# Two padded bias vectors fetched in four strided requests each instead of sixteen

## The chip, the cores and the metric

The kernel runs on one core of one Trainium2 chip. The metric is the device time of that core in microseconds (us), as the median of several runs. The profile comes from one further execution; its span and its own time are given beside the median.

## The reference

Two layers, each an attention over a context followed by a routed feed-forward part, work on `x` (4 batches, 512 tokens, 256 features) and a context of the same shape. All values are 32-bit floats. Cut to its frame:

```python
x = x + _L0_xattn_ref(_layernorm(x), ctx, ctx, ...)   # attention over probability vectors, then an MLP of 1024
x = x + _L0_ffn_ref(_layernorm(x), ...)               # 8 experts of 1024, the best two of each token
x = x + _L1_xattn_ref(_layernorm(x), ctx, ctx, ...)   # 16 heads of 16 features
x = x + _L1_ffn_ref(_layernorm(x), ...)               # 8 experts of 512, the best one of each token
```

The two vectors of this case belong to the third line:

```python
qw = split_heads(q @ Wq + bq)
kw = split_heads(k @ Wk + bk)
```

Each has 256 entries, 16 for each of 16 heads.

## The kernel before, in words

Tokens lie on the 128 partitions, four to a partition for each batch. At the start the function loads x and context of batch 0, the weights and biases that the first stages need, and then the other batches, one request after the other on the queue of SyncE (SP): `load_batch(0)`; `packed("Wk_pad")` and `rows("L1_xattn_Wv")` (L124); `packed_column("bk_pad")` and the bias of values (L125); `load_batch(1)` (L126); `WdT`, `b_diff`, the columns of the layer norm, the MLP's weights `w1_mlp` and `w2_mlp`, further biases, and batches 2 and 3 (L127 to L139). A later group, `load_later` (L141 to L152), loads what only layer 1 uses: `Wq_pad`, `packed_column("bq_pad")`, `wo` in 16 requests of 16 rows (L150), `w_red` and `wg` (L151).

On the host the biases are laid out for heads of 32 places: place 0 is kept for something else, places 1 to 16 hold the head's 16 entries, the rest is zero. The padded 512 places are turned into a source of 128 rows and 4 columns, so that head `hd` lies in column `hd // 4`, at rows `32 * (hd % 4) + 1` and on. `packed_column` (L105) brings them into a tile `w` of 128 partitions and 2 columns without the padding. It does so head by head: 16 requests of 16 rows with one element each.

Layer 0 works by batches. `front` (L685) normalizes x (`q`), makes probability vectors of q and of the context (`qp`, `kp`, through L657 to L664), their logarithms (`ql`, `kl`, L666), and the differences (L699, L702); GpSimd (POOL) adds `b_diff` to q (L700). `attend` (L705) transposes the differences on TensorE (`transposed`, L258, with copies at L267 and L269), multiplies them (`pm_sid`, L721), takes the exponential (L722), weighs the context (`pf`, L729) and multiplies by `WdT` (`pd`, L744, added to q as `f` at L745). `perceive` (L748) is the MLP; POOL adds `ln_b` to x (L754) and `b2_mlp` to f (L753). `remember` (L879) is the part of layer 1 that needs only the context: it transposes the context (L899), multiplies by `Wk` (L905), adds the bias of keys on ScalarE (ACT, L906), multiplies by `Wv` (L915), adds the bias of values on VectorE (DVE, L919), and stores keys and values in DRAM (L910, L923). `select_weights` (L809) turns `wg` and `w_red` into the weights of layer 1's selection: four small DVE operations on `wg` (L813, L814, L815, L817) with a power on POOL (L816), and then TensorE. `clear` (L195) fills the DRAM buffers `sent` with rows that go nowhere: 32 stores (L199).

What sets the order: in the first stage (L938 to L951), over batch 0 and the start of batch 1, the order on TensorE (PE), DVE, ACT and POOL is that of the program. From L952 to L987 a scheduler orders the instructions of all engines by its own estimates of times, until the tail of layer 0 and layer 1's attention again fix the order on PE. SP's queue is ordered by the scheduler throughout. Each engine, SP too, works through its own queue in order. A transfer signals its end on one of eight semaphores, which are used in turn; so in the built program a request on SP waits until the eighth request before it has landed.

The bias of queries `bq` is used only in layer 1 (`prepare`, L1128).

Of the kernel before, what the change touches and what calls it, by code (L numbers as in the profile page):

```python
# [21 lines left out]
P = 128  # L22
NT = S // P
NC = D // P
# [3 lines left out]
HEADS, DH = 16, 16  # L28
# [15 lines left out]
def xattn_ffn_kernel(ctx: ExitStack, tc: tile.TileContext, a: dict, out: bass.AP):  # L44
    nc = tc.nc
# [59 lines left out]
    def packed_column(name):  # L105

        w = const.tile([P, NC], F32, tag=name, name=name)
        for hd in range(HEADS):
            c, r = divmod(hd * DH, P)
            g, j = divmod(hd, 4)  # L110
            nc.sync.dma_start(w[r : r + DH, c : c + 1], a[name][32 * j + 1 : 32 * j + 1 + DH, g : g + 1])
        return w

    def load_w1(ap, n):
# [8 lines left out]

    (wk, pack_wk), wv = packed("Wk_pad"), rows("L1_xattn_Wv")  # L124
    bk, bv = packed_column("bk_pad"), spread_row("L1_xattn_bv")  # L125
    load_batch(1)  # L126
    wdT = rows("WdT")  # L127
# [13 lines left out]
    def load_later():  # L141

        w_out, b_out = rows("L0_ffn_W_out"), spread_row("L0_ffn_b_out")
        (wq, pack), bo = packed("Wq_pad"), spread_row("L1_xattn_bo")
        pack()
        bq = packed_column("bq_pad")
        wo = const.tile([P, NC, D], F32, tag="wo", name="wo")
        for hd in range(HEADS):
            c, r = divmod(hd * DH, P)
            nc.sync.dma_start(wo[r : r + DH, c, :], a["Wo_pad"][32 * hd + 1 : 32 * hd + 1 + DH, :])  # L150
        w_red, wg = rows("L1_ffn_w_red", RED), columns("L1_ffn_wg")  # L151
        return w_out, b_out, wq, bo, bq, wo, w_red, wg  # L152
# [525 lines left out]
    with tc.tile_pool(name="l0a", bufs=2) as lp, tc.tile_pool(name="l0tmp", bufs=2) as tp, tc.tile_pool(  # L678
        name="l0mid", bufs=1
    ) as midp, tc.tile_pool(  # L680
        name="l0p_m", bufs=3, space=bass.MemoryType.PSUM
# [276 lines left out]
        for b in range(B):  # L958
# [9 lines left out]
            if b < B - 1:  # L968
# [7 lines left out]
                if b == B - 2:  # L976
                    ((e, row),) = send.pick(1)
                    w = send.weights(e)
# [169 lines left out]
    with tc.tile_pool(name="f0tmp", bufs=2) as tp, tc.tile_pool(  # L1148
        name="f0mid", bufs=2
    ) as midp, tc.tile_pool(  # L1150
        name="f0p_m", bufs=3, space=bass.MemoryType.PSUM
# [31 lines left out]
    with tc.tile_pool(name="l1a", bufs=2) as lp, tc.tile_pool(name="l1s", bufs=1) as sp, tc.tile_pool(  # L1183
        name="l1p_s", bufs=6, space=bass.MemoryType.PSUM
# [268 lines left out]
    with tc.tile_pool(name="f1tmp", bufs=2) as tp, tc.tile_pool(  # L1453
        name="f1mid", bufs=2
    ) as midp, tc.tile_pool(
        name="f1p_m", bufs=3, space=bass.MemoryType.PSUM
# [60 lines left out]
```

## Time and profile before

| | us |
|---|---|
| median of 3 runs | 1018.66 (1017.84 to 1022.89) |
| the profiled execution, its time | 1020.77 |
| the profiled execution, its span | 1019.0 |
| PE busy | 957.3 |
| DVE busy | 530.1 |
| ACT busy | 358.0 |
| POOL busy | 290.9 |
| mean granted clock of PE | 0.979 |
| 16 requests of `bk_pad` on SP | 10.15, from 3.18 |
| 15 of the 16 requests of `bq_pad` on SP | 7.94, from 42.11 |

Times in the text are microseconds from the start of the span. "SPq" is the time that SP's sequencer spends on issuing a request, its waits among it; the landing of a transfer is seen at the first instruction that waited for it. "PEclk" or "granted clock" is the share of its full clock that PE was given. A line of the program stands for all instructions that it makes; `x16` counts them.

### The profile page before, as it was taken

How to read it: one execution, taken by the hardware profiler on the slowest of the kernel's cores; microseconds unless marked ns; L12 is line 12 of the kernel's file. 1: busy time of each engine (PE TensorE's matmuls, PEld its weight loads, DVE VectorE, ACT ScalarE, POOL GpSimd, SP SyncE). 2: the span in 40 equal slices, each digit the busy share in tenths (PEclk: the TensorE clock that was granted, in tenths of full speed). 3: DMA queues.
4: the chain of work that ended last, by engine and by line, in shares of the span. 5: the costliest groups of instructions: out<-in, count | busy, mean ns of one | idle time of the engine just before them, and what ended most of it. 6: DMA issues, size and time to landing. Idle time of an engine off the chain costs nothing. (4 is left out here: it accounts for less than half of the span.)

```text
span 1019.0 us, 14212 instructions
## 1 busy us (share of the span) xinstructions
PE 957.3 (94%) x4885; PEld 645.4 (63%) x4885; DVE 530.1 (52%) x1409; ACT 358.0 (35%) x647; POOL 290.9 (29%) x333
## 2 busy tenths in 40 slices
PE   5979989999898999999999989999999999997996
PEld 3556757676777888888888864343333343346785
DVE  6775595456762222222323158676687777624232
ACT  4535242122121122111222203655656555563231
POOL 3330143325341222211112146306023220123543
PEclk9889999999999999999999999999999999999998
DMA  6779999973333655666655331101011102035672
GB/s 198 232 185 246 249 252 240 246 172 114 130 125 130 212 183 170 206 213 211 230 163 199 123 139 43 27 12 43 5 38 47 43 6 99 37 87 166 203 226 79
DMA packets 113713, 146.05 MB, mean 143 GB/s; under 512 B 15060, under 2 KB 95197, under 8 KB 113632
## 3 DMA queue, kind: packets, MB, share of 16 engines
q1 hardware_dynamic: 106592, 128.19, 44.4%
q0 software_dynamic: 6624, 15.80, 4.8%
q8 instruction: 43, 0.70, 0.3%
q10 hardware_dynamic: 416, 1.05, 0.3%
q14 instruction: 38, 0.31, 0.1%
HBM read 86.71 MB, written 58.80 MB: 143 GB/s over the span
## 5 line engine op out<-in xcount | busy, mean ns | idle before, releaser
L1218 DVE TENSOR_REDUCE nm<-sc 128x1 f32<-128x512 f32 x256 | 165.1, 683 | 61.4 <-PE scT L1211 57.5
L1215 ACT ACTIVATE ex<-scT 128x512 f32<-128x512 f32 x256 | 138.5, 596 | 94.7 <-PE scT L1211 94.0
L634 PE MATMUL pm<-inT,w 128*128 128x256 f32 x736 | 166.9, 382 | 3.1 <-ACT mid L638 2.4
L647 PE MATMUL po<-w,mid 128*128 128x256 f32 x736 | 163.3, 379 | 0.0
L1211 PE MATMUL sc<-kT,qT 32*128 32x512 f32 x512 | 154.5, 650 | 3.8 <-DVEq L626 1.6
L634 PEld LDWEIGHTS pm<-inT,w 128*128 128x128 f32 x736 | 140.1, 192 | 24.5 <-ACT mid L638 4.4
L647 PEld LDWEIGHTS po<-w,mid 128*128 128x128 f32 x736 | 138.0, 190 | 17.8
L1211 PE MATMUL scT<-qT,kT 32*128 32x512 f32 x512 | 148.5, 639 | 0.9 <-ACT ex L1215 0.9
L523 POOL DMA_INDIRECT came<-y,rows x38 | 37.5, 986 | 223.8 <-DVE y L601 223.8
L244 POOL TENSOR_TENSOR rstd<-var,halved 128x4 f32<-128x4 f32 (+1 forms) x32 | 28.1, 883 | 248.9 <-DVE var L243 243.0
L601 DVE SCALAR_TENSOR_TENSOR y<-po,rows,y 128x256 f32<-128x256 f32 x54 | 26.1, 484 | 130.4 <-PE po L647 125.6
L638 ACT ACTIVATE mid<-pm,b 128x256 f32<-128x256 f32 x108 | 49.8, 471 | 110.5 <-PE pm L634 85.5
L1211 PEld LDWEIGHTS sc<-kT,qT 32*128 32x128 f32 x512 | 50.4, 185 | 59.0 <-DVE nm L1218 35.8
L636 DVE TENSOR_SCALAR mid<-pm,b 128x256 f32<-128x256 f32 x76 | 36.8, 484 | 95.5 <-PE pm L634 91.3
L598 ACT ACTIVATE y<-b,rows 128x256 f32<-128x256 f32 x54 | 24.5, 500 | 158.2 <-DMA b<-in_L_ffn_b 125.1
L339 POOL DMA_INDIRECT sent<-rows,slot x48 | 47.4, 987 | 102.6 <-DVE slot L336 62.1
L1232 PE MATMUL av<-ex,va 128*32 128x512 f32 x512 | 68.6, 605 | 0.0
L763 PE MATMUL pm<-hT,w 128*128 128x512 f32 x128 | 62.4, 612 | 0.5 <-DVE hT L676 0.5
L769 PE MATMUL po<-w,mid 128*128 128x256 f32 x256 | 59.2, 381 | 0.0
L769 PEld LDWEIGHTS po<-w,mid 128*128 128x128 f32 x256 | 47.9, 190 | 9.1 <-issue 3.1
L1211 PEld LDWEIGHTS scT<-qT,kT 32*128 32x128 f32 x512 | 45.5, 183 | 6.4 <-issue 4.6
L1232 PEld LDWEIGHTS av<-ex,va 128*32 128x32 f32 x512 | 10.2, 108 | 48.2 <-issue 36.8
(312 smaller groups left out, 1268.4 us busy)
## 6 DMA issues: line engine op xcount, KB each, us to landing
w<-in_L_ffn_W SPq DMA_DIRECT2D x40, 1024.0 KB
sent<-nowhere SPq DMA_DIRECT2D x32, 1161.0 KB
w<-in_L_ffn_W SPq DMA_DIRECT2D x22, 512.0 KB
rows<-sent SPq DMA_DIRECT2D x27, 258.0 KB
b<-in_L_ffn_b SPq DMA_DIRECT2D x28, 128.0 KB
y<-came SPq DMA_DIRECT2D x6, 512.0 KB
x<-in_x SPq DMA_DIRECT2D x4, 512.0 KB
c<-in_ctx SPq DMA_DIRECT2D x4, 512.0 KB
```

What stands on the lines that cost most here:

```text
L339: i = nc.gpsimd.indirect_dma_start(out=sent[self.layer][:, :], out_offset=bass.IndirectOffsetOnAxis(ap=slot[:, t - tts[0], k : k + 1], axi ...
L523: i = nc.gpsimd.indirect_dma_start(out=came[self.layer][:, :], out_offset=bass.IndirectOffsetOnAxis(ap=rows[:, u, TO:ROW].bitcast(I32), ax ...
L634: nc.tensor.matmul(pm, w1[:, c, ts(k, P)], inT[:, c, :], start=c == 0, stop=c == NC - 1)
L636: nc.vector.tensor_scalar(mid[:, k, :], pm, bias[:, k : k + 1], 0.0, ALU.add, ALU.max)
L638: nc.scalar.activation(mid[:, k, :], pm, func, bias=bias[:, k : k + 1])
L647: nc.tensor.matmul(po, mid[:, k, ts(t, P)], w2[:, k, :], start=k == 0, stop=k == n - 1)
L763: nc.tensor.matmul(pm, w1_mlp[:, c, ts(k, P)], hT[:, c, :], start=c == 0, stop=c == NC - 1)
L769: nc.tensor.matmul(po, mid[:, k, ts(t, P)], w2_mlp[:, k, :], start=k == 0, stop=k == HD // P - 1)
L1211: nc.tensor.matmul(sc, stay, move, start=True, stop=True)
L1215: nc.scalar.activation(ex, sc, AF.Exp, scale=1.0 / DH**0.5)
L1218: nc.vector.tensor_reduce(nm[:, t, head, 0:1], sc, AX.X, ALU.max, negate=True)
L1232: nc.tensor.matmul(av[32 * head : 32 * head + 32, :], vas[b % 2][:, t, 4 * g + head, :], exs.pop((t, head)), start=t == 0, stop=t == NT - 1,)
```

## The change

The source is seen as columns `c` and halves `g`, and each request takes the 64 rows that go to one half of one column of the tile: for each of four heads (`j`) its 16 entries (`r`, places 1 to 16). One request so has 64 rows of one element, four requests make a bias, and `bk_pad` and `bq_pad` are both fetched in this way. The 256 elements and the tile are the same.

```diff
         w = const.tile([P, NC], F32, tag=name, name=name)
-        for hd in range(HEADS):
-            c, r = divmod(hd * DH, P)
-            g, j = divmod(hd, 4)
-            nc.sync.dma_start(w[r : r + DH, c : c + 1], a[name][32 * j + 1 : 32 * j + 1 + DH, g : g + 1])
+        of_heads = a[name].rearrange("(j r) (c g) -> c g j r", r=32, g=2)
+        for c in range(NC):
+            for g in range(2):
+                nc.sync.dma_start(w[64 * g : 64 * g + 64, c : c + 1], of_heads[c, g, :, 1 : 1 + DH])
         return w
```

In the built program PE and ACT keep their order. On SP four requests stand where sixteen stood, and the store of values of batch 1 (L923), which stood behind fifteen of the sixteen `bq_pad` requests, now stands behind the four and eleven of the `wo` requests. On DVE the operations L813, L814, L815 and L817 move from around L799 to L806 to the place behind the last L664 of batch 2's `kp`, among the four L745 of batch 1; one bn_stats of batch 2 (L241), its aggregate and the variance (L243) move the other way, to behind L805. On POOL, L816 moves ahead of the two operations that stood before it.

## The prediction, made before the changed kernel was run

> **What bounds the kernel now.** I read the page first, then the sums by 20 us stretches, then the timelines of SP, PE, DVE, ACT and POOL over the first 80 us, the waits of PE, and last the order of the instructions in the two built kernels. On the page PE is the bound:
>
> ```profile
> span 1019.0 us, 14212 instructions
> PE 957.3 (94%) x4885; PEld 645.4 (63%) x4885; DVE 530.1 (52%) x1409; ACT 358.0 (35%) x647; POOL 290.9 (29%) x333
> ```
>
> A change to small loads can only win where PE stands still, and over the span PE waits for a transfer three times: twice for context (12.0 us together: 7.2 at the start, 4.8 here) and once for routed rows (2.8 us, at 313 us, far from this change). The 4.8 us lie directly behind the biases of keys. The timeline of SP's queue (start, duration, issue, count):
>
> ```profile
> 1.27 0.70 SPq L64 DMA_DIRECT2D c<-in_ctx  x1
> 2.67 0.47 SPq L78 DMA_DIRECT2D L_xattn_Wv<-in_L_xattn_Wv  x1
> 3.18 10.15 SPq L111 DMA_DIRECT2D bk_pad<-in_bk_pad  x16
> ...
> 13.84 0.43 SPq L63 DMA_DIRECT2D x<-in_x  x1
> 14.32 0.57 SPq L64 DMA_DIRECT2D c<-in_ctx  x1
> 14.93 0.62 SPq L78 DMA_DIRECT2D WdT<-in_WdT  x1
> 15.59 0.82 SPq L90 DMA_DIRECT2D L_xattn_b_diff<-in_L_xattn_b_diff  x1
> ```
>
> Sixteen requests hold SP for 10.15 us, and from 8.5 to 13.5 us the DMA engines are 0.04 busy. The context of batch 1 is asked for at 14.32 and PE gets it at 21.54, as PE's timeline shows (in brackets the idle time before, and who ended it):
>
> ```profile
> 13.14 3.62 PE L915 MATMUL pv<-L_xattn_Wv,kc 128*128 128x256 f32 x16
> 21.54 1.94 PE L899 MATMUL psTr<-ident,c 128*128 128x128 f32 x8 [4.79 <-DMA c<-in_ctx]
> 23.28 1.92 PE L263 MATMUL psTr<-ident,qp 128*128 128x128 f32 x8
> 25.87 1.97 PE L263 MATMUL psTr<-ident,ql 128*128 128x128 f32 x8 [0.68 <-ACT dT L267]
> 27.77 3.42 PE L721 MATMUL pm_sid<-dT,lT 128*128 128x512 f32 x4
> ```
>
> **Part 1, the biases of keys.** Twelve requests of 10.15 / 16 = 0.63 us go: 7.6 us of SP. Not all of it comes through. In the built program every request on SP waits for the landing of the eighth before it (the trace shows such waits: 1.4 us for the context and 1.0 us for Wk among the sixteen). So x of batch 1 is now held by context 0, which landed at about 7.1 (ACT began on it at 7.10), and context 1 by Wk (POOL began on it at 8.48). Context 1 is thus issued at 8.5 in place of 14.3, and with the same 7.2 us to landing it is there at 15.7, before PE's pv ends at 16.76. The 4.79 us wait goes.
>
> What is late next is DVE. Its rows for batch 0: L699 ends at 19.54, L702 at 20.67, two L919 at 21.87; only then comes the copy of dT (0.69), to 22.6. The eight transposes of ql need that buffer: 1.9 us, to 24.5, and pm_sid starts there in place of 27.77. First gain: **3.3 us**, not 4.8.
>
> Part of it is given back by something the trace shows one batch later:
>
> ```profile
> 39.09 3.24 DVE L664 TENSOR_SCALAR kp<-kp,pr_r 128x256 f32<-128x256 f32 x4
> ...
> 39.71 2.47 POOL L700 TENSOR_TENSOR q<-q,L_xattn_b_diff 128x1024 f32<-128x1024 f32 x1 [2.88 <-ACT qp L657]
> ```
>
> The same four DVE operations take 1.14 us at 12.60 and at 16.05; under a POOL add they take 3.24. Today the first such add (b_diff onto q of batch 0) waits 10.2 us for its data, to 22.71, and meets only copies out of PSUM, which keep their 0.69. With b_diff issued at about 9.7 and landing 5 to 7 us later (now 7.1), the add starts between 14.7 and 16.8 and falls on L661 to L664 of qp (15.63 to 17.19). Everything from there to dT waits for its end: add at 14.7: 1.4 us; at 15.6: 2.3; after 17.2: nothing. Bounds 0 and 2.4, taken 1.8. So **1.5 us** are left of 3.3.
>
> A rule and a row for the clock. From 20.5 to 30.5 the granted clock was 0.50, which is why four pm_sid matmuls took 3.42 us. The Trainium skill, "TensorE: Matmul & The Clock Gate", Part 1, says that an idle stretch of about 3.4 us halves the clock: by it, closing the gap keeps the clock, and ql's transposes (0.9) and pm_sid (1.7) would win 2.6 us more. But the row says that transposes do not hold it: they ran from 21.54 to 27.7 with the clock at 0.50 throughout, and Part 4 of the page says the same of transpose mode. Between pv and pm_sid there are only transposes in either kernel, so I take no gain; 2.6 stays as the far end. There is a loss too: the clock came back at 30.7, 2.9 us after pm_sid began; if it comes back at fixed instants, as five drops (20.4, 64.8, 136.8, 194.8, 314.0) lying multiples of about 3.4 us apart suggest, an earlier pm_sid works longer at half clock. Plus or minus 1.7 us (half of 3.4), taken as 0.
>
> **The new requests themselves** (64 rows of one element) have no row. Near ones: requests of 128 rows were issued in 0.33 (b_mlp_col) to 0.71 us (ln_b_col), those of 16 in 0.31 to 0.65, so issue does not grow with the rows: 0.5 taken, bounds 0.3 and 2.5 (four times 0.63). The skill's "DMA: Bandwidth & Descriptors", section "Why a DMA increments its semaphore by 16 and not by 1", speaks against the change: a request is spread over the largest number up to 16 that divides the outer dimension of both sides. Source 4 x 16 against 64 rows gives 4 DMA engines with 16 elements each, where a 16-row request had 16 with one each. The row: ten old requests in 5 us at 0.04 busy on 16 engines are 3.2 us of engine time for 160 elements, 0.02 us each; 16 in a row are 0.3 us and all 64 of a bias on one engine 1.3. By the row that is hidden: the first use (ACT L906 at 11.63) comes 2 to 3 us after their landing behind Wv. Cost 0, at most 1.
>
> **Part 2, the biases of queries.** They are first used at 566 us; only the queue behind them matters:
>
> ```profile
> 42.11 7.94 SPq L111 DMA_DIRECT2D bq_pad<-in_bq_pad  x15
> 50.15 0.37 SPq L923 DMA_DIRECT2D values<-room  x1
> ...
> 51.04 8.08 SPq L150 DMA_DIRECT2D wo<-in_Wo_pad  x16
> ...
> 59.63 0.42 SPq L84 DMA_DIRECT2D L_ffn_wg<-in_L_ffn_wg  x1
> ```
>
> Twelve go at 0.53: 6.3 us. The store of values now stands behind eleven of the wo requests instead of fifteen bq; it waits for DVE (room L919, ends 48.88), which is 1.5 earlier. The 32 clearing stores begin at about 51 in place of 60.16 and last 150 us; no compute engine waits for them on the page, so this is worth nothing.
>
> The built order holds one surprise: the scheduler moves the four small DVE operations on wg (and POOL's power of them, L816) from about 67 us to just after L664 at 54.95. DVE works in order, so it now waits there for wg, and behind it stand the four f (L745) for which POOL rstd, h and PE wait. When is wg there? values at 47.4, five wo (0.5 each), w_red, wg: issued about 51, landed about 53 to 54. DVE comes at 55.8 - 1.5 = 54.3. In time, by 0.3 to 1.3 us. Cost of the operations: 0.15 + 0.12 + 0.13 + 0.21, and 0.3 of waiting for POOL (0.54 against a stats of 0.39 in between), less a stats and its aggregate (0.48) moved out: **+0.4 us**. Those, moved behind L805, hold var and rstd of batch 2 back by 1.3 us; q keeps ahead of ACT's L657 (72.71), but POOL's next two adds slide over DVE's L659 to L664 (73.79 to 78.7), and `turned` (L824), for which PE waits at 78.5, comes 0.5 late: **+0.5 us** (0 to 0.9). PE, ACT and everything after 80 us keep their order and move along; PE is over 9 tenths busy there.
>
> **Sum.** -3.3 + 1.8 + 0.4 + 0.5 = -0.6 us. The profiled execution took 1020.77 (span 1019.0 and 1.77 around it): 1020.2. It lies 2.1 above the median of the runs, 1018.66; from that, **1018.1**.
>
> **Rivals.**
> - *The gain survives* (0.24). b_diff lands after 17.2, or the DVE costs vanish: 1018.66 - 3.3 + 0.2 = 1015.6. For it: the transfers of batch 1 run at 380 GB/s and share the engines. Against: b_diff was 7.1 us from issue to use. With a clock that also returns one step earlier (1.7 to 2.6) it is 1013 to 1014.
> - *DVE stands at wg* (0.09). If a request of 64 rows costs SP four of the old ones, wg is issued at 59.6 as now and lands at 61.8: 61.8 - 54.3 = 7.5 us of stall, 1025.6. It decides once wg lands later than about 60.0; between 54.3 and there the time only slides up within half a per cent. Against: the issue rows of 128-row requests.
> - *Nothing is saved at the start* (0.13): the eighth-before rule holds context 1 up to its old time; what is left are the DVE costs: 1018.66 + 0.9 = 1019.6. Against: Wk and context 0 landed by 8.5.
> - The forecast itself 0.54.
>
> **How the numbers follow.** About 0.5% (5.1 us) is what a measurement of this kernel can tell from no change; the three runs lie 5.05 us apart. Faster by more (under 1013.6) is the clock end of the first rival: 0.09. Slower by more (over 1023.75) is the second: 0.09. Within: 0.82. Range: down to the first rival with part of a clock step (1013.8), up to a wg that is 4 us late (1022.4).
>
> **What would show it.** Right: four L111 in 2 to 2.5 us from 3.2, context 1 issued near 8.5, no wait of PE for it at 16.8; POOL's first L700 near 15 to 16 with DVE L664 of qp stretched to 2 to 3 us; pm_sid starting near 26; wg_sq without a wait near 54. Wrong: L664 of qp at 1.14 (then the first rival), wg_sq waiting for DMA (the second), L111 over 1.5 us each, or a clock at 1.00 between 20 and 27 us.

## The result, and the profile after

The changed kernel takes 1018.07 us (median of 21 runs, 1012.24 to 1024.89). The kernel before, run in turn with it on the same chip, took 1022.89 (21 runs, 1015.97 to 1027.78): a ratio of 0.995, 95% interval 0.9926 to 0.9973. That is 5.1 us less, with an interval of 2.8 to 7.6. The predicted level, 1018.1, was met; the predicted difference was not. The forecast took 0.6 us off a median of three runs that lay some 4 us lower than that of 21 runs. So the question for the experiments is where 5 us came from when the sum gave 0.6.

The profiled execution of the changed kernel took 1023.91 us, more than most of its runs, at a mean granted clock of 0.972 (before: 1020.77 at 0.979). Its place in time is therefore read at marks inside the span, not at its end. The page's first lines:

```profile
span 1022.2 us, 14180 instructions
PE 964.1 (94%) x4885; PEld 645.9 (63%) x4885; DVE 528.8 (52%) x1409; ACT 357.7 (35%) x647; POOL 290.9 (28%) x333
```

PE is busy for 6.8 us more than before with the same instructions. Nearly all of that lies in one place, and it is the clock: from 600 to 624 us the mean granted clock is 0.64 here and was 0.93 before, which makes 7.0 us of those 24. SP's timeline of the changed kernel:

```profile
3.18 2.61 SPq L111 DMA_DIRECT2D bk_pad<-in_bk_pad  x4
7.15 0.35 SPq L63 DMA_DIRECT2D x<-in_x  x1
8.79 0.61 SPq L64 DMA_DIRECT2D c<-in_ctx  x1
10.11 0.47 SPq L90 DMA_DIRECT2D L_xattn_b_diff<-in_L_xattn_b_diff  x1
36.00 2.44 SPq L111 DMA_DIRECT2D bq_pad<-in_bq_pad  x4
45.70 0.35 SPq L923 DMA_DIRECT2D values<-room  x1
49.25 0.38 SPq L84 DMA_DIRECT2D L_ffn_wg<-in_L_ffn_wg  x1
```

The requests follow as forecast: context 1 at 8.79 (8.5 said), b_diff at 10.11 (9.7 said), wg at 49.25. One request of 64 rows costs 0.65 us where one of 16 cost 0.63. x of batch 1 is issued (7.15) when ACT begins on context 0 (7.16), context 1 (8.79) when POOL begins on Wk (8.83): this fits the wait for the eighth request before each, as forecast. ACT's first use of `bk_pad` (L906, at 13.02) waits for PE, so the landing of the new requests is hidden. PE, POOL and DVE of the changed kernel at the start:

```profile
21.92 1.09 PE L263 MATMUL psTr<-ident,qp 128*128 128x128 f32 x8 [2.89 <-DVE qp L699]
23.69 2.28 PE L263 MATMUL psTr<-ident,ql 128*128 128x128 f32 x8 [0.68 <-ACT dT L267]
25.76 3.62 PE L721 MATMUL pm_sid<-dT,lT 128*128 128x512 f32 x4
```

```profile
16.31 2.53 POOL L700 TENSOR_TENSOR q<-q,L_xattn_b_diff 128x1024 f32<-128x1024 f32 x1 [3.59 <-DMA L_xattn_b_diff<-in_L_xattn_b_diff]
...
38.20 2.88 POOL L700 TENSOR_TENSOR q<-q,L_xattn_b_diff 128x1024 f32<-128x1024 f32 x1 [5.36 <-ACT qp L657]
```

```profile
16.26 3.25 DVE L664 TENSOR_SCALAR qp<-qp,pr_r 128x256 f32<-128x256 f32 x4
...
37.12 1.14 DVE L664 TENSOR_SCALAR kp<-kp,pr_r 128x256 f32<-128x256 f32 x4
```

The wait for context 1 is gone, and a wait for DVE stands in its place. POOL's first add falls on L664 of qp, which takes 3.25 us in place of 1.14, as forecast. pm_sid starts at 25.76 in place of 27.77: 2.0 us. This pair of traces makes that step look large, though. In the five other traces with the start of before (among the experiments below) pm_sid starts at 25.15 to 26.88, and in the three others with the keys in four requests and POOL's add in its place at 25.47 to 26.50: at this point the gain is not clear of the spread.

The last DVE line is what the forecast did not follow. Before, L664 of kp of batch 1 was the one that took 3.24 us, under POOL's second add. Now it starts 2.0 us sooner, and is done at 38.26, just as that add begins; the add then holds one small operation instead (L661, 0.95 us in place of 0.17). PE meets the difference where it waits for the bias of values (`room`), which DVE adds behind these operations. Before:

```profile
46.59 2.01 PE L729 MATMUL pf<-c,es 128*128 128x258 f32 x8 [1.62 <-DVE room L919]
```

and after:

```profile
45.82 3.73 PE L729 MATMUL pf<-c,es 128*128 128x258 f32 x16 [0.44 <-DVE room L919]
```

With a second wait of 0.43 us at 49.03 this made 2.05 us before; it is 0.44 now. What the first collision took is given back by the second, which no longer happens. The transposes that follow (`neg`) start at 49.38 in place of 52.59, 3.2 us sooner. In the same traces as above they start at 48.79 to 49.08 with the keys in four and at 50.82 to 52.64 with the start of before: here the gain is clear of the spread.

The next difference lies at the bias that the first layer's gate needs. PE, DVE and POOL before:

```profile
67.08 1.23 PE L802 MATMUL pb<-ident,b_all 128*128 128x128 f32 x4 [3.03 <-DVE lT L269]
```

```profile
62.48 1.38 DVE L254 TENSOR_SCALAR h<-f,mv,rstd 128x256 f32<-128x256 f32 x4 [0.81 <-POOL rstd L244]
64.14 2.29 DVE L791 COPY b_all<-b_in_col 128x256 f32<-128x256 f32 x1 [0.28 <-issue]
```

```profile
63.94 2.34 POOL L753 TENSOR_TENSOR f<-f,L_xattn_b 128x1024 f32<-128x1024 f32 x1 [1.50 <-DVE h L254]
```

and PE, DVE and POOL after:

```profile
61.88 0.71 PE L802 MATMUL pb<-ident,b_all 128*128 128x128 f32 x4 [1.04 <-DVE lT L269]
...
72.69 0.61 PE L828 MATMUL pw<-turned 16*128 16x8 f32 x4 [1.49 <-DVE turned L824]
```

```profile
60.93 0.29 DVE L791 COPY b_all<-b_in_col 128x256 f32<-128x256 f32 x1
```

```profile
61.02 2.40 POOL L753 TENSOR_TENSOR f<-f,L_xattn_b 128x1024 f32<-128x1024 f32 x1 [1.50 <-DVE h L254]
```

Before, DVE paused for 0.28 us ahead of the copy b_all, POOL's add began 0.20 us before the copy, and the copy took 2.29 us. After, there is no pause, the copy takes 0.29 us and is all but done when the add begins, and PE waits 1.04 us in place of 3.03. At pb PE is 5.2 us ahead. Before, the granted clock was 0.50 from 66 to 70 us, behind the wait of 3.03 us; after, it is 1.00 there, and PE is 7.4 us ahead when pm_sid is done (69.83 in place of 77.26). It then waits 1.49 us for `turned`, where it waited for nothing (0.5 was said), the clock falls (0.55 from 74 to 76 us), and of the lead 4.2 us are left at 130 us.

Marks on PE, before and after: psGate of the first tile 134.41 and 130.23; psGate of batch 2's second look, 241.74 and 237.56; the rank at 257.78 and 253.60; the first scores of layer 1 (L1211) at 598.06 and 596.14. So 4.2 us are held from 130 to 254 us. At 310 us a wait for routed rows takes 4.10 us where it took 2.85; 1.9 us are left at the first scores, and the clock from 600 us on takes the rest in this execution.

### The profile page after: what moved, and what is told of

It is laid out like the page before. It is cut to its first block, busy times and chain, and to the rows that moved or that the text cites. A ratio compares the mean times of both kernels' runs of the same rounds, so it can differ in the third digit from the quotient of the medians.

```text
span 1022.2 us, 14180 instructions
## 1 busy us (share of the span) xinstructions
PE 964.1 (94%) x4885; PEld 645.9 (63%) x4885; DVE 528.8 (52%) x1409; ACT 357.7 (35%) x647; POOL 290.9 (28%) x333
## 5 line engine op out<-in xcount | busy, mean ns | idle before, releaser
L1211 PE MATMUL sc<-kT,qT 32*128 32x512 f32 x512 | 158.4, 677 | 3.2 <-DVEq L626 1.6
L1211 PE MATMUL scT<-qT,kT 32*128 32x512 f32 x512 | 151.2, 650 | 0.9 <-ACT ex L1215 0.9
L1211 PEld LDWEIGHTS sc<-kT,qT 32*128 32x128 f32 x512 | 50.8, 193 | 59.8 <-DVE nm L1218 34.6
L1211 PEld LDWEIGHTS scT<-qT,kT 32*128 32x128 f32 x512 | 45.7, 186 | 6.3 <-issue 4.6
```

What stands on the lines that cost most here:

```text
L1211: nc.tensor.matmul(sc, stay, move, start=True, stop=True)
```

## The experiments

Theory: two DVE operations came out from under POOL's adds (kp at 37 us, b_all at 61 us), and that is what the sum lacked. The rivals: SP's time, that is the earlier clears (L199, from 49.72 in place of 60.16), has a share after all; or it is the clock. How far the clock goes: the span of a run times what its mean granted clock lacks of 1 gives at most what the run lost to it. Over the runs of one kernel this loss goes with the time (correlation 0.88 over 51 runs of the kernel before, with a loss of 25.9 us on average; the time grows by 0.63 us for each us of it). Differences of under 2 us are therefore hardly seen here, with some 20 runs each. Each group of runs has the kernel before in it, on the same chip; the runs down to one_request_add are two groups on one chip, the others two groups on another.

**bk_only** fetches only the keys in four; DVE and POOL keep the order of before.

```diff
+        if name == "bk_pad":
             of_heads = a[name].rearrange("(j r) (c g) -> c g j r", r=32, g=2)
             ...
+        else:
             for hd in range(HEADS):
             ...
```

> Only the biases of keys in four requests; those of queries keep sixteen, and DVE and POOL keep the order of the kernel before. If the gain is made at the start (theory): context 1 is issued near 8.8 us, PE does not wait for it, pm_sid of batch 0 starts near 25.8 in place of 27.8, the four L664 of batch 1's kp take 1.14 us, and the time is 3 to 5 us below the kernel before. If the gain comes from the queue behind the biases of queries (rival), pm_sid may move but the time stays within 1 us of the kernel before.

**bq_only** has the same split for `bq_pad`; DVE and POOL take the order of the changed kernel.

> Only the biases of queries in four requests; DVE and POOL have the order of the changed kernel. Theory: pm_sid of batch 0 starts at 27.8 as before, wg is issued near 53 and the time lies within 1.5 us of the kernel before, with the costs of the moved wg operations (0.4 and 0.5) in it. Rival (the gain comes from this half): 3 to 5 us below the kernel before.

Measured: bk_only 1016.29 against 1022.92, ratio 0.9924 (0.9891 to 0.9956); bq_only 1017.89, ratio 0.9948 (0.9922 to 0.9973). Each half alone wins, and the halves do not add: both together are at 0.995. PE in bq_only, at the start and at pb:

```profile
20.87 1.06 PE L905 MATMUL psTr<-ident,c 128*128 128x128 f32 x8 [3.44 <-DMA c<-in_ctx]
...
64.82 0.71 PE L808 MATMUL pb<-ident,b_all 128*128 128x128 f32 x4 [1.04 <-DVE lT L275]
```

The wait for context 1 is still there, and the wait ahead of pb is the short one. In bk_only it is the reverse: no wait for context 1, pm_sid at 26.50, kp's L664 at 1.14 us, and 3.03 us ahead of pb. So the two effects belong one to each half. The forecast that the half of the queries is worth nothing had missed.

**ball_act_before** is the kernel before with one line changed: ACT makes the copy b_all.

```diff
-            nc.vector.tensor_copy(b_all, b_in.unsqueeze(2).to_broadcast([P, NC, P]))
+            nc.scalar.copy(b_all, b_in.unsqueeze(2).to_broadcast([P, NC, P]))
```

> The kernel before with one change: the copy b_all (L791) is made by ACT and not by DVE. Theory: in the kernel before this copy fell under POOL's add of b2_mlp and took 2.29 us, and in the changed kernel it took 0.29 because it came first by a hair; without it on DVE, PE's wait of 3.0 us before pb falls to about 1 us, the clock does not drop at 64.8, and the time is 2 to 3.5 us below the kernel before. Rival: the copy of lT behind it would wait for POOL in any case, PE's wait stays at 2.5 us or more and the time is the same.

Measured: 1021.63 against 1022.92, ratio 0.9994 (0.9969 to 1.0019). The wait ahead of pb fell to 0.55 us and psGate of the first tile came at 130.47, 3.9 us sooner; 1.8 us of that were there ahead of the copy (the transposes of neg at 50.82), by a start that was quicker in this trace. Yet nothing of the 2 to 3.5 us that were expected was left at the end: PE waited 2.29 us at 242.47 for xn, where it had not waited before, and the rank came at 258.51. An early win alone does not reach the end. This is taken up again below.

**add_on_dve** is the changed kernel with the first b_diff add made by DVE in `attend`, so that POOL does not meet L664 of qp.

```diff
-            nc.gpsimd.tensor_tensor(q, q, per_token(b_diff), ALU.add)
+            if b:
+                nc.gpsimd.tensor_tensor(q, q, per_token(b_diff), ALU.add)
 ...
+            if b == 0:
+                nc.vector.tensor_tensor(q, q, per_token(b_diff), ALU.add)
```

> The changed kernel, with batch 0's add of b_diff made by DVE behind the copy of lT and not by POOL. Theory: the four L664 of qp fall from 3.25 to 1.14 us, pm_sid of batch 0 starts near 24.0 to 24.5 in place of 25.8, and the time is 1 to 2 us below the changed kernel, 5 to 7 below the kernel before. Rival (clock or another wait takes it back): pm_sid earlier, but the stage from 31 us on where it is in the changed kernel, and the time as the changed kernel's.

Measured: 1014.45 against 1022.92, ratio 0.991 (0.9875 to 0.9945). Its DVE and PE:

```profile
15.59 1.14 DVE L664 TENSOR_SCALAR qp<-qp,pr_r 128x256 f32<-128x256 f32 x4
```

```profile
19.14 1.09 PE L263 MATMUL psTr<-ident,qp 128*128 128x128 f32 x8 [1.02 <-DVE qp L699]
...
22.67 1.98 PE L724 MATMUL pm_sid<-dT,lT 128*128 128x512 f32 x4
```

L664 is back at 1.14 us, pm_sid starts 3.1 us sooner than in the changed kernel, and four of its matmuls take 1.98 us in place of 3.62: here the clock did not halve, as the sums by stretches show (the last columns are the granted clock, the DMA share and GB/s):

```profile
19.00:21.00 2.00, 1.18 (x9) 0.95 (x10) 2.00 (x4) 0.58 (x1) 0.00 (x0) 1.00 1.09 366
21.00:23.00 2.00, 1.49 (x9) 1.04 (x10) 2.00 (x4) 0.23 (x1) 0.00 (x0) 1.00 1.09 318
```

PE's wait ahead of qp's transposes is 1.02 us here against 2.89. The first collision is real, and its price at the start is as the forecast had it. But the marks at 130 to 254 us are only 1.0 to 1.4 us ahead of the changed kernel's, since the second collision is back. POOL's add of batch 1 now starts at 33.17 and meets kp:

```profile
33.31 3.15 DVE L664 TENSOR_SCALAR kp<-kp,pr_r 128x256 f32<-128x256 f32 x4
```

and PE waits 2.46 us for `room` at 40.89, in place of 0.44. It is the same in bk_add and one_request_add below (3.15 and 3.17 us).

**clears_late** is the changed kernel with sixteen requests for `bq_pad`, now behind wg, so that the clears start later again.

```diff
         w_red, wg = rows("L1_ffn_w_red", RED), columns("L1_ffn_wg")
+        for hd in range(HEADS):
+            c, r = divmod(hd * DH, P)
+            g, j = divmod(hd, 4)
+            nc.sync.dma_start(bq[r : r + DH, c : c + 1], a["bq_pad"][32 * j + 1 : 32 * j + 1 + DH, g : g + 1])
```

> The changed kernel, with the biases of queries fetched once more in sixteen requests behind the load of wg; nothing else moves but SP's queue, so the 32 clearing stores begin about 8 us later (near 58 in place of 49.7). Theory (the clears end where the scatters of routed rows are sent, so an earlier PE only pays if the clears are earlier too): PE is where it is in the changed kernel up to 130 us, then the wait for xn near 190 us grows by 1 to 2 us and a further one of about 2 us appears near 240; the time is 2 to 4 us above the changed kernel. Rival (clears are hidden, as the prediction said): the same time as the changed kernel within 1 us.

Measured: 1014.72 against 1021.71, ratio 0.993 (0.990 to 0.996). The clears ran from 56.72 to 205.65. It is not slower than the changed kernel, and PE waits nowhere near 240 us. The 2 to 4 us above the changed kernel that were expected did not come. Taken by itself this says that the start of the clears is hidden.

**bk_add** is bk_only with the add on DVE.

> Only the biases of keys in four requests, and batch 0's add of b_diff on DVE. Theory: qp's four L664 take 1.14 us, pm_sid starts near 23 to 24; the DVE order is that of the kernel before, so PE's 3 us wait before pb stays; the time is 1 to 2 us below the kernel with only the biases of keys, 8 to 10 below the kernel before. Rival: the early gain is lost at the clears, and the time is that of the kernel with only the biases of keys.

Measured: 1015.53, ratio 0.9935 (0.9909 to 0.9961). L664 of qp is at 1.14 and psGate of the first tile 2.6 us ahead of bk_only, but the times of the two kernels cannot be told apart.

**one_request** and **one_request_add** have both biases without padding in the source, one request of 128 rows each; the second with the add on DVE too.

```diff
-        of_heads = a[name].rearrange("(j r) (c g) -> c g j r", r=32, g=2)
-        ...
+        nc.sync.dma_start(w, a[name])
```

> The host lays the two biases out without padding, as 128 rows of two elements, and each is fetched in one request. x of batch 1 is then the seventh request and waits for nothing: x issued near 4.3, context 1 near 4.8 us, both landed by 12. Theory: PE's next wait is for qp in any case, and POOL's add of b_diff moves to 10 to 13 us, where it stretches one of the DVE steps by up to 2 us: pm_sid near 25 to 26, the time within 2 us of the changed kernel, either side. Rival (SP's time is what counts): another 3 us below the changed kernel. The scheduler's order differs in 11 lines on PE, which may cost or win about 1 us.

> One request for each bias, and batch 0's add of b_diff on DVE. Theory: as the changed kernel with that add on DVE, pm_sid near 22.7, time 8 us below the kernel before, since DVE sets the start once the add is gone. Rival: further below, 10 us or more, as the clears begin earlier still (near 46).

Measured: 1010.61, ratio 0.9909 (0.9876 to 0.9942), and 1009.02, ratio 0.9899 (0.9871 to 0.9927). The first request costs SP 0.47 us, and context 1 is issued at 5.33. The scheduler puts pm_sid of batch 1 ahead of pb, so that PE no longer waits there. A time within 2 us of the changed kernel was expected of the first; since the order on PE changed too, the two runs do not tell what the time of SP alone is worth. The second is the fastest kernel of the study: 10 us below before, and below the changed kernel by 5 us going by the ratios, by 9 going by the medians, which were taken in different groups of runs.

**order_alone** asks for what its name says: all biases in sixteen requests as before, but `w_red` and `wg` between the fourth and the fifth request for `wo`. The scheduler then orders DVE and POOL exactly as in the changed kernel. **bk_ball_act** is bk_only with the copy b_all on ACT.

```diff
         for hd in range(HEADS):
             c, r = divmod(hd * DH, P)
+            if hd == 4:
+                w_red, wg = rows("L1_ffn_w_red", RED), columns("L1_ffn_wg")
             nc.sync.dma_start(wo[r : r + DH, c, :], a["Wo_pad"][32 * hd + 1 : 32 * hd + 1 + DH, :])
-        w_red, wg = rows("L1_ffn_w_red", RED), columns("L1_ffn_wg")
```

> Before, with all biases in sixteen requests as before, but w_red and wg asked for between the fourth and the fifth request for wo, so that the scheduler puts DVE and POOL in exactly the order of the changed kernel (L813 to L817 behind the last L664 of kp of batch 2, b_all ahead of POOL's add L753). No request is saved anywhere. Theory 1, the half of the queries works only through DVE's order: like the kernel with only the queries in four, 3 to 6 us below before (ratio 0.994 to 0.997), b_all at 0.29 us and PE's wait ahead of pb near 1.0 in place of 3.03, while PE still waits for context 1 at the start (3.4 to 4.8 us). Theory 2, the half of the queries works by the seconds that SP wins (earlier store of values, earlier clears): clears as late as before (near 60), so within 1.5 us of before. Theory 3, chance: ratio around 1.000.

> Only the keys in four requests (DVE and POOL in the order of before), and the copy b_all made by ACT in place of DVE. If the 3.03 us wait ahead of pb is a loss that reaches the end: 2 to 4 us below the kernel with only the keys in four (ratio 0.988 to 0.991 in place of 0.992), PE's wait ahead of pb near 0.5 and psGate of the first tile 2 to 3 us earlier than 131.4. If it is made up for later, as it was when the same copy was moved in the kernel before: ratio 0.992 to 0.993, psGate of the first tile earlier, but the transposes of the rank (253 to 256 us) not.

Measured: order_alone 1018.41 against 1020.39, ratio 0.9987 (0.9966 to 1.0009); bk_ball_act 1012.16, ratio 0.9929 (0.9902 to 0.9956). In order_alone all local marks of the order are there (b_all 0.29 us, 1.04 us ahead of pb, psGate of the first tile at 131.72), and again little is left. In bk_ball_act the wait ahead of pb is 0.55 us and the first psGate 2.7 us sooner than in bk_only, and PE waits 2.25 us at 237.72; 1.7 us of the 2.7 are left at the rank (253.76 against 255.45).

Three kernels now wait near 240 us. What they share: in each trace the clears took long, 163 to 164 us from the first to the last request (150 us in the trace of before), and PE's look at xn came 18.0 to 18.3 us after the last clearing request had left SP (241.61 against 223.36, 242.47 against 224.44, 237.72 against 219.44). In the eleven other traces PE came 20.0 us or more after it, and waited for nothing there. So order_alone was run again, as **order_alone_2**, beside **order_early_clears**, in which the last twelve requests for `wo` become two, with no other difference in the order of the four engines.

```diff
+        for c, r, rows_n in (*((0, hd * DH, DH) for hd in range(4)), (0, 4 * DH, P - 4 * DH), (1, 0, P)):
+            if r == 4 * DH:
+                w_red, wg = rows("L1_ffn_w_red", RED), columns("L1_ffn_wg")
+            nc.sync.dma_start(wo[r : r + rows_n, c, :], a["Wo"][c * P + r : c * P + r + rows_n, :])
```

> The kernel with DVE's order alone once more. In every trace so far PE's last look at xn of batch 2 (psGate near 240 us) comes no earlier than 18.0 to 18.3 us after the last clearing request left SP, and the clears took either 149 to 153 us or 162 to 165 us from the first to the last. Theory 1, the clears are a second bound that PE has to wait for when it is early and the clears are slow: if the clears take 162 us or more here, PE waits about 2 us again near 241 and the time is within 0.3% of before; if they take 153 us or less, no wait there and 3 to 5 us below before (ratio 0.995 to 0.997). Theory 2, the waits near 241 have another cause: the wait is there, or not, whatever the length of the clears.

> The kernel with DVE's order alone, but the twelve requests for wo that stand between wg and the clears become two (one of 64 rows, one of 128, from a source without padding; the same numbers). The order on PE, DVE, ACT and POOL is the same. The clears start near 55.5 in place of 60.5. Theory 1: their end and with it the earliest psGate near 240 comes 5 us sooner, so there is no wait of over 0.5 us near 241 even with slow clears, and the gain of the order reaches the end: 3 to 5 us below before (ratio 0.995 to 0.997) and, with slow clears, 2 to 4 us below order_alone_2. Theory 2: no difference to order_alone_2 beyond 1 us, and the same waits.

Measured: order_alone_2 1014.61 against 1017.49, ratio 0.9966 (0.9944 to 0.9989); order_early_clears 1017.62, ratio 0.999 (0.9966 to 1.0013). The same kernel, traced twice. POOL and PE of order_alone, with the clears from 60.54 to 223.36:

```profile
228.25 1.04 POOL L340 DMA_INDIRECT sent<-rows,slot  x1 [0.18 <-issue]
...
237.34 0.14 POOL L304 IOTA rows<- 128x4 int32 x1 [4.26 <-DMA sent<-rows,slot]
```

```profile
241.61 0.78 PE L851 MATMUL psGate<-ident,xn 128*128 128x128 f32 x4 [2.06 <-DVE xn L255]
```

and of order_alone_2, with the clears from 59.71 to 210.39:

```profile
228.47 1.04 POOL L340 DMA_INDIRECT sent<-rows,slot  x1 [0.18 <-issue]
...
233.81 0.14 POOL L304 IOTA rows<- 128x4 int32 x1 [0.50 <-DMA sent<-rows,slot]
```

```profile
239.74 0.78 PE L851 MATMUL psGate<-ident,xn 128*128 128x128 f32 x4
```

Up to POOL's scatter the two executions are 0.2 us apart. In the first, the scatters land late behind the clears, POOL waits 4.26 us before it can number the next rows, and behind that wait stand rstd on POOL, xn on DVE and psGate on PE. In the second POOL waits 0.50 us, and PE is still 2.0 us ahead of before. From 225 to 230 us the DMA engines were busy throughout in the first (a share of 1.09 by the view) and idle in the second (0.00). The times of the two groups do not tell them apart (their intervals overlap); the traces do. So the clears are a second chain: the compute chain comes about 18 us behind their last request at the earliest. In the trace shown, the kernel before reached that point 31.7 us after its quick clears; with clears of 164 us it would have been 241.74 - 60.16 - 164 = 17.6 us, right at the limit. By this account, with slow clears any gain ahead of 240 us is lost unless the clears start earlier too, which is what the change's saved requests also do (49.72 in place of 60.16). clears_late met quick clears (149 us) and could not show this. order_early_clears met quick clears as well: no wait, as either theory has it, but also no gain in time. It lost 25.0 us to the clock on average and order_alone_2 23.0, each give or take 1.0; with the whole loss taken off they agree (992.2 and 992.1). Its expectation of 3 to 5 us below before was a miss. What makes the clears quick or long was not found; all traces of one group of runs were of one kind, each of the two chips had a group of either kind, and between 60 and 200 us the quick ones moved 244 to 250 GB/s and the long ones 228 to 231 in the traces.

## Why the prediction was right and wrong

- **Level and difference.** 1018.1 was met by luck: the forecast took 0.6 us off for a change that was worth 5.1 (2.8 to 7.6), and took it off a median that was 4.2 us too low; from the median of 21 runs it would have said 1022.3. The sign was right.
- **Biases of keys, the queue.** Right: twelve requests saved 7.5 us of SP, context 1 came 5.5 us sooner, the wait of 4.79 us went, DVE was late next, 64-row requests cost what 16-row requests cost.
- **-3.3 + 1.8 at the start.** Right in mechanism: the collision took 2.1 us (3.25 less 1.14), and pm_sid came 2.0 us sooner where 1.5 was said. The size is less sure than that: the trace that the sum was read from has the latest pm_sid of the six with this start, and by the means of the six and of the four with the keys in four (26.48 and 26.05) it is 0.4 us. add_on_dve shows that without the collision pm_sid comes 5.1 us sooner than in that trace, not 3.3, and at full clock. For the changed kernel "I take no gain" by the clock was right: its wait of 2.89 us was there, and pm_sid ran at half clock: the clock fell at 23.0, 4.0 us after that wait began, with nothing but transposes since its end. But the reason was too strong. In add_on_dve, bk_add and one_request_add the clock stayed at 1.00 from 16 to 26 us, with nothing but transposes and waits of 1.1 us or less between pv and pm_sid. So transposes did not bring a lost clock back, and with short waits it was not lost; for that case the end of 2.6 us that the prediction kept for the clock was nearer (pm_sid came 1.8 us sooner than the 3.3 and took 1.4 us less than before).
- **The step that failed first**: the sum treated the collision with POOL's add as new, though the row it was read from was that of an add one batch later, and did not ask what the shift does to that row. It went from 3.24 to 1.14: a missing term of 2.1 us on DVE, which bk_only shows too, and of 1.6 us at PE (waits for `room` of 2.05 and 0.44). Where the add of batch 0 was taken off POOL, the row went back to 3.15 us and the wait with it.
- **The step that failed second**: "so this is worth nothing", of the biases of queries, with +0.4 and +0.5 for the moved operations. DVE's new order brought the copy b_all ahead of POOL's add L753: a missing term of 2.0 us at PE (3.03 to 1.04). It was no chance of one execution: the copy took 2.28 or 2.29 us, behind a pause of 0.28, in the three traces with the old order (before, bk_only, bk_add) and 0.29 us without a pause in the seven with the new one; why the order takes the pause away is open. The +0.4 was 0.3 on DVE (h comes 2.9 us sooner where 3.2 was the lead) and nothing at PE. The +0.5 at `turned` was 1.49 us in the trace of the changed kernel, where PE had run pm_sid at full clock, and nothing in those of bq_only, clears_late and order_alone, where the clock fell ahead of it. Whether the gain of the order reaches the end depends on the clears by the traces, not yet by the times: the four runs with the order, or the copy moved, and without the keys' half (order_alone twice, order_early_clears, ball_act_before) measure 0.1 to 0.3% less than before (of them only order_alone_2 is clear of no change), bq_only 0.5%.
- **"No compute engine waits for them on the page"**, of the clears, was true of that page and wrong as a price: in three traces POOL's L303 and so PE wait 2.1 to 2.3 us behind clears that end late.
- **The rivals.** "The gain survives" came nearest in its size (3.1 us, to 1015.6), but not by its reason: b_diff did not land after 17.2, and DVE's costs did not vanish. "DVE stands at wg" did not come: wg_sq ran at 52.52 without a wait. "Nothing saved at the start" fell with context 1 at 8.79.
- **The whole.** That each half moves PE is shown, each by marks of its own. How the 5.1 us divide between them is not: either half alone measures as much as both (0.9924, 0.9948 and 0.995), within the intervals. The marks at the first scores (596 us) say 1.9 us for the changed kernel, 2.7 for bk_only and 2.6 for bq_only, against one trace of before. But clears_late, which has both halves and the order of the changed kernel, is 5.9 us ahead there: among other things, its clock was 1.00 from 70 to 80 us, where that of the changed kernel's trace fell to half. So one trace of the changed kernel cannot decide whether the halves add. Behind 596 us no instruction changed, and the traces differ by the clock.

## What to carry to other kernels

When a change shifts one engine's work against another's, list every place where the two now collide, and every place where they no longer do: the same 2.1 us were lost at 16 us and won back at 37. A slow side chain that nobody waits for can still be what comes next: compute how far behind it the main chain runs, at its longest seen duration, before you price its head start at nothing. And a forecast of a level needs as many runs of the kernel before as the difference needs; three of them were 4 us off.

## What the runs showed that was not expected

- A POOL add of 128 x 1024 held some of DVE's operations in SBUF almost for its whole length: four tensor_scalars of 1.14 us took 3.25, a copy of 0.29 us took 2.29. A copy that started 0.1 us ahead of the add escaped it (60.93 against 61.02), and a tensor_reduce under the add of 38.20 kept its 1.22 us (L660, 38.90).
- The clears, 32 stores of 1.16 MB, took 149 to 153 us or 162 to 165 us for the same stores.
- The runs of one unchanged kernel spread over 12 to 15 us, and the loss by the granted clock goes with most of it (correlation 0.88 to 0.91 in the four groups of the kernel before).
